# A selective-scan network on one core: the starting value of each bank of sums comes from ScalarE instead of TensorE

## The chip, the cores and the metric

The kernel runs on one NeuronCore of one Trainium2 chip. The metric is the device time in microseconds (us) of one execution of the whole network. One execution has also been taken by the hardware profiler; its trace gives start, length and releaser of every instruction. The engines are named PE (TensorE, matrix products), PEld (its weight loads), DVE (VectorE), ACT (ScalarE), POOL (GpSimd) and SP (the queue that issues most DMAs).

## What is computed

The network has four layers on a 4 x 56 x 56 x 96 image. Layers 0 and 1 are state-space layers: a 192-channel sequence of L = 3136 tokens is run through a selective scan in four directions (along the rows or along the columns, each forward and reversed), and the four results are added. Layers 2 and 3 are attention and a small feed-forward net. What matters here is the scan, cut from the reference:

```python
def step(h, inp):
    dA_l, dBu_l, C_l = inp
    h = dA_l * h + dBu_l                                  # per channel d and state n (16 states)
    return (h, jnp.einsum('bkdn,bkn->bkd', h, C_l))       # sum over the 16 states
_, ys = jax.lax.scan(step, h0, (dA, dBu, Ct))
return jnp.moveaxis(ys, 0, -1) + u * Dp[None, :, :, None] # the skip term
...
y = jnp.transpose(y1 + y2 + y3 + y4, (0, 2, 1)).reshape(Bsz, Hh, Ww, DINNER)
```

So for each direction a sum over 16 states is formed, the four directions are added up, and `u * D` is added (for all four directions at once it is `u` times the sum of the four D, in layer 0 weighted by a softmax).

## The kernel before

**Rounds.** The scans of the two layers, the four images, the four directions and the seven chunks of 448 tokens are one long list of *rounds* (`scans`, from line 604). A chunk has eight rounds, r = 0 to 7: two halves of the channels (e = 0, 1; 96 channels each) times four quarters of the states (q = 0 to 3). There are 2 x 4 x 4 x 7 x 8 = 1792 rounds. The order of the instructions is written out by hand: every engine runs its own list in the order in which Python emits it.

In one round n these are emitted:

- DVE: two products `h <- du, b` (line 695), then three scans (line 702), one for each group of 32 channels; further elementwise work of the other lanes stands between.
- ACT: three exponentials `da` into three PSUM banks (`decay`, line 654), each for the next round; group g can be written only when scan g of this round has read the bank. Two small copies carry the scan's state from chunk to chunk (`kept` line 672, `carried` line 667).
- POOL: one product `h <- du, cb` (line 690) and the product with C, `hc <- h, cb` (line 744).
- PE: `b`, the row of B spread over partitions (line 597, `begin`), for the next round. There is one bank for it, so it waits for this round's two products. Then `add_up` (line 764): four products of `hc` with a 0/1 matrix `four` (line 775), which add the sums over states of round n - 2 to the bank `y`. Two rounds lie between a scan and its sum: the list `late`.

**The bank `y`.** It gathers four rounds (q = 0 to 3), 96 channels x 448 tokens. There is one such bank. Before the change, `add_up` of q = 0 starts it: a product of the identity with Y (the running sum of the directions), or in the first direction of U with the diagonal matrix `skip` (line 771, `start=True`), which overwrites the bank. Two products with a zero matrix follow (line 772), then the four sums. After q = 3 `keep_sums` (line 779) copies the bank back to Y on ACT (line 782). Since `keep_sums` of one half and the start of the next use the same bank, line 771 waits for line 782. In terms of r, `keep_sums` stands in rounds r = 1 and r = 5, and the start of the next bank in r = 2 and r = 6. There are 448 such changes of bank.

**Directions.** In the directions along the columns (`orient` = 1) Y and U are read and written with a stride of 56 elements. Two of the four directions of each layer are of that kind; the first, which reads U, never is.

**Zeros.** `keep_busy` (line 754) puts products with a zero matrix on PE so that each round has about the same amount of work on it: `WARM` = 6.8 units less what the planner has counted for the round in `self.work`. It does nothing in the rounds with q = 0. It is called ahead of `begin`, so these zeros stand ahead of `b` in PE's list. They write into the bank `y`, adding nothing.

**The other lanes.** All other parts of the network (projections, convolutions, feed-forward nets) are generators that are advanced between the pieces of a round (`overlap`, line 935). A planner decides by `spend` and `room` (lines 965 and 973) whether a piece fits: it keeps a backlog for ACT and PE, reduced by `SPARE` each half round, and bounded by `ACT_LIMIT` and `PE_LIMIT`. The list `strided` (line 718) books the product of line 771 as 1.5 units of PE, or 3.0 in a strided direction. After the last round, what is left of the lanes runs alone (the *tail*).

Of the kernel before, what the change touches and what calls it, by code (L numbers as in the profile page):

```python
# [11 lines left out]
F32 = mybir.dt.float32  # L12
# [3 lines left out]
AF = mybir.ActivationFunctionType  # L16
# [4 lines left out]
HS = 56  # L21
L = HS * HS
C = 96
DI = 192
NS = 16
NE = 2
NG = 3
NQ = 4
# [4 lines left out]
CS = 448  # L33
# [16 lines left out]
WARM, PER_P = 6.8, 1.6  # L50
# [116 lines left out]
class Net:  # L167
# [82 lines left out]
    def setup(self):  # L250
        nc, tc, const = self.nc, self.tc, self.const
# [46 lines left out]
        w = const.tile([128, 4], F32, name="wts")  # L298
# [15 lines left out]
        for l in range(2):  # L314
            dv = par("c128", f"{l}D")[:C].rearrange("p (e k) -> p e k", e=NE)
            s = const.tile([C, NE], F32, name=f"dsum{l}")
            if l == 0:
                dw = const.tile([C, NE, 4], F32, name="dw")
                nc.vector.tensor_tensor(dw, dv, w[:C].unsqueeze(1).to_broadcast([C, NE, 4]), ALU.mult)
                dv = dw  # L320
            nc.vector.tensor_reduce(s, dv, AX.X, ALU.add)
            g = const.tile([C, NE, C], F32, name=f"skip{l}")
            for e in range(NE):
                nc.vector.tensor_scalar_mul(g[:, e], self.ident[:C, :C], s[:, e : e + 1])
            self.skip.append(g)


        bn = {}
        for n, bias in (("bn1", "1dw_b"), ("bn2", "1pw_b")):
            s = const.tile([C, 1], F32, name=n + "s")  # L330
# [273 lines left out]
    def scans(self):  # L604

        nc, sp = self.nc, self.sp
        chunks = []
        for l in range(2):
            for i in range(NB):
                for n, (orient, rev) in enumerate(ORDER[l]):
                    for step in range(NCS):
                        ch = Step()
                        ch.l, ch.i, ch.orient, ch.rev, ch.step = l, i, orient, rev, step
                        ch.k = 2 * orient + rev if l == 0 else orient + 2 * rev  # L620
                        ch.c = NCS - 1 - step if rev else step
                        ch.n, ch.first = n, n == 0 and step == 0
                        ch.skip = n == 0
                        ch.last = n == 3 and step == NCS - 1
                        ch.cb, ch.dt, ch.du = [], [], []
                        chunks.append(ch)
        rounds = [(ch, e, q) for ch in chunks for e in range(NE) for q in range(NQ)]
        per = NE * NQ


        da = [self.psum.tile([128, 512], F32, name=f"da{g}")[:, : CS + 4] for g in range(NG)]
        for t in da:
            nc.vector.memset(t, 0.0)

        def steps(n):

            return [(ch, n - per * j) for j, ch in enumerate(chunks[max(0, n // per) : n // per + 3], max(0, n // per))]

        def ahead(n):
            for ch, o in steps(n):  # L640
                self.on_tensor(ch, o)

        for n in range(-14, 0):
            for ch, o in steps(n):
                self.prepare(ch, o)
            for ch, o in steps(n):
                self.prepare_on_scalar(ch, o)
            ahead(n)

        def decay(n, g):  # L650

            if n < len(rounds):
                ch, e, q = rounds[n]
                nc.scalar.activation(da[g][:, INNER], ch.dt[e][:, g], AF.Exp, scale=ch.par.na[:, e, q, g : g + 1])  # L654

        def column(t, at):

            return t[:, at : at + 2 * ROW + 1 : ROW]

        def carried(n):  # L660

            if n < len(rounds):
                ch, e, q = rounds[n]
                hs[n] = sp.tile([128, WIDE], F32, name="h", bufs=3)
                if not ch.step:
                    return
                nc.scalar.copy(column(hs[n], ROW if ch.rev else 1), ch.par.carry[:, e, q])  # L667

        def kept(n):
            ch, e, q = rounds[n]  # L670
            if ch.step < NCS - 1:
                nc.scalar.copy(ch.par.carry[:, e, q], column(hs[n], 2 if ch.rev else CS + 1))  # L672

        def own(n):
            ch, e, q = rounds[n]
            return NQ * e + q in (OWN_TAIL if ch.l and ch.i else OWN)

        hs, bs = {}, {}

        def tokens(t):  # L680

            return self.groups(t, 2)[:, :, :CS]

        def begin(n):

            if n < len(rounds):
                ch, e, q = rounds[n]
                bs[n] = self.spread_b(ch, q)
                if not own(n):
                    nc.gpsimd.tensor_tensor(tokens(hs[n])[:, 2], ch.du[e][:, 2], ch.cb[q][:, 1], ALU.mult)  # L690

        def products(n):
            ch, e, q = rounds[n]
            for g in range(3 if own(n) else 2):
                nc.vector.tensor_tensor(tokens(hs[n])[:, g], ch.du[e][:, g], bs[n], ALU.mult)  # L695

        def scan(n, g):
            ch, e, q = rounds[n]
            c = 1 if ch.step else 0
            way = slice(CS + 1 + c, 1, -1) if ch.rev else slice(2 - c, CS + 2)  # L700
            h = hs[n][:, g * ROW :]
            nc.vector.tensor_tensor_scan(h[:, way], da[g][:, way], h[:, way], 0.0, ALU.mult, ALU.add)  # L702

        carried(0)
        carried(1)
        begin(0)
        self.exp_and_ln()
        self.tables = True
        for g in range(NG):
            decay(0, g)  # L710
        late = []
        for n, (ch, e, q) in enumerate(rounds):
            r = NQ * e + q
            products(n)
            for c, o in steps(n):
                self.prepare(c, o)
            self.half_round()
            strided = [1.5 + 1.5 * ch.orient] * (r % NQ == 2)
            strided += [1.5 + 1.5 * c.orient for c, o in steps(n) for _ in self.projected(c, o)]
            self.spend((0.6, 0.7, 1.7, 0, 0, 0, 0.7, 0.6)[r], (1.3, 1.3, 0, 0, 0, 0, 0.4, 0.4)[r] + sum(strided))  # L720
            yield "F", n, r
            for c, o in steps(n):
                self.prepare_on_scalar(c, o)
            ended = late.pop(0) if len(late) == 2 else None
            if ended:
                self.keep_busy(ended[2])
            begin(n + 1)
            if ended:
                self.add_up(*ended)
            ahead(n)  # L730
            self.half_round()
            for g in range(NG):
                if g == 1:
                    yield "C", n, r
                if g == 2 and ended and ended[2] == NQ - 1:
                    self.spend(0.6, 0)
                    self.keep_sums(*ended[:3])
                scan(n, g)
                if g == 2:
                    kept(n)  # L740
                decay(n + 1, g)
            carried(n + 2)
            hc = sp.tile([128, NG, CS], F32, name="hc", bufs=3)
            nc.gpsimd.tensor_tensor(  # L744
                hc, tokens(hs[n]), ch.cb[q][:, 0].unsqueeze(1).to_broadcast([128, NG, CS]), ALU.mult,
            )
            late.append((ch, e, q, hc))
            del hs[n], bs[n]
        for ended in late:
            self.add_up(*ended)  # L750
        self.keep_sums(ch, e, q)
        yield "C", len(rounds), 0

    def keep_busy(self, q):

        if q:
            self.add_zeros(int(max(0.0, WARM - self.work) + 0.5))
        self.work = 0.0

    def add_zeros(self, n):  # L760
        for _ in range(n):
            self.nc.tensor.matmul(self.y[:C], self.zeros, self.some, start=False, stop=False)  # L762

    def add_up(self, ch, e, q, hc):

        nc = self.nc
        if q == 0:
            self.y = self.psum.tile([128, 512], F32, tag="y", name="y", bufs=1)[:, :CS]
            o = self.y[:C].rearrange("p (a b) -> p a b", b=HS)
            a, w = (self.U[e], self.skip[ch.l][:, e]) if ch.skip else (self.Y[e], self.ident[:C, :C])  # L770
            nc.tensor.matmul(o, w, self.in_order(a, ch.orient, ch.c * CS, CS), start=True, stop=False)  # L771
            self.add_zeros(2)

        for n, g in enumerate((0, 1, 2, 2)):
            nc.tensor.matmul(  # L775
                self.y[32 * n : 32 * n + 32], self.four, hc[:, g], start=n == 3, stop=n == 3 or q == NQ - 1,
            )

    def keep_sums(self, ch, e, q):

# [591 lines left out]
```

## Time and profile before

| | us |
|---|---|
| median of 3 runs | 8356.53 (8340.41 to 8364.75) |
| the profiled execution, time | 8364.46 |
| the profiled execution, span from first to last instruction | 8362.7 |
| outside the span | 1.8 |
| first round starts / last scan ends (timeline) | 111.8 / 7983.9 |
| tail after the last scan | 378.8 |

| engine | busy us | share | instructions |
|---|---|---|---|
| PE | 7469.6 | 89% | 33633 |
| PEld | 2721.6 | 33% | 33633 |
| DVE | 7516.6 | 90% | 9555 |
| ACT | 6109.8 | 73% | 12807 |
| POOL | 7177.3 | 86% | 3991 |

A row of the page's table of groups names the source line, the engine, the operation, what it writes and reads (`out<-in`) and its shape; then the busy time in us and the mean length of one in ns; then the idle time of that engine just before these instructions and what ended most of it. A product of fp32 operands shows as two records in this trace (14336 records of line 775 for 1792 x 4 products). The mean granted clock of PE is 0.898 of full speed; in the record it is either full or half.

### The profile page before, as it was taken

The page shows a single profiled execution, that of the slowest core. Times are in us where ns is not written, and L with a number is a line of the kernel's source. Part 1 is how long each engine was busy: PE and PEld are TensorE (multiplying, and loading weights), DVE is VectorE, ACT ScalarE, POOL GpSimd, SP SyncE. Part 2 cuts the span into 40 slices and gives each one's busy share as a digit, 9 for nine tenths or more (in the row PEclk, how much of TensorE's full clock was granted, in tenths as well). Part 3 has the DMA queues.
Part 4 walks back from the last instruction along what each step waited for, and adds up shares of the span by engine and source line. Part 5 has one row for each costly group of instructions (what it writes and reads, how often), then busy time and mean ns, then how long its engine had stood idle before and what let it go on. Part 6 is the DMA issues. An engine that isn't in the chain of part 4 may idle for free. (4 is left out here: it accounts for less than half of the span.)

```text
span 8362.7 us, 119228 instructions
## 1 busy us (share of the span) xinstructions
PE 7469.6 (89%) x33633; PEld 2721.6 (33%) x33633; DVE 7516.6 (90%) x9555; ACT 6109.8 (73%) x12807; POOL 7177.3 (86%) x3991
## 2 busy tenths in 40 slices
PE   7889888898889988898899979988899888998997
PEld 3333233232333223232322323333333333333344
DVE  5999999999998999999998999999999999999921
ACT  5778878776787768786777766777776777767736
POOL 4999989989998999899898998998888888889820
PEclk8899989899999989998898989988899888999986
DMA  5777777678766777677776777676766667666721
GB/s 154 179 188 189 203 179 182 167 175 199 178 174 170 172 188 181 172 177 184 177 175 167 174 185 176 166 170 172 186 166 162 166 173 182 167 160 167 175 57 48
DMA packets 944159, 1417.77 MB, mean 170 GB/s; under 512 B 169410, under 2 KB 936644, under 8 KB 942628
## 3 DMA queue, kind: packets, MB, share of 16 engines
q1 hardware_dynamic: 942720, 1408.34, 68.2%
q8 instruction: 264, 4.33, 0.2%
q14 instruction: 403, 3.30, 0.1%
q10 hardware_dynamic: 772, 1.80, 0.1%
HBM read 1141.42 MB, written 268.14 MB: 169 GB/s over the span
## 5 line engine op out<-in xcount | busy, mean ns | idle before, releaser
L702 DVE TENSOR_TENSOR_SCAN h<-da,h 128x449 f32<-128x449 f32 (+1 forms) x5376 | 5507.1, 1071 | 134.9 <-ACT da L654 79.3
L744 POOL TENSOR_TENSOR hc<-h,cb 128x1344 f32<-128x1344 f32 x1792 | 4884.8, 2726 | 598.8 <-DVE h L702 413.6
L654 ACT ACTIVATE da<-dt,na 128x448 f32<-128x448 f32 x5376 | 3353.1, 632 | 1143.2 <-DVE h L702 1104.4
L695 DVE TENSOR_TENSOR h<-du,b 128x448 f32<-128x448 f32 x3584 | 2019.6, 604 | 182.7 <-PE b L597 112.6
L775 PE MATMUL y<-hc,four 128*32 128x448 f32 x14336 | 1913.0, 609 | 17.8 <-POOL hc L744 17.4
L690 POOL TENSOR_TENSOR h<-du,cb 128x448 f32<-128x448 f32 x1792 | 1754.1, 979 | 141.4 <-DMA cb<-cd 110.1
L762 PE MATMUL y<-w,zeros 128*96 128x448 bf16 x4843 | 1354.0, 397 | 0.0
L597 PE MATMUL b<-cf,sel 128*128 128x448 bf16 x1792 | 680.2, 380 | 631.2 <-DVE h L695 626.6
L762 PEld LDWEIGHTS <-zeros 128*96 128x96 bf16 x4843 | 603.2, 135 | 1111.0 <-issue 965.1
L775 PEld LDWEIGHTS y<-hc,four 128*32 128x32 f32 x14336 | 294.2, 113 | 1182.5 <-issue 660.5
L433 PE MATMUL pp<-U,wd 96*128 96x448 f32 x896 | 664.5, 830 | 12.1 <-DMA U<-u 8.3
L771 PE MATMUL y<-Y,ident 96*96 96x448 f32 x672 | 542.9, 898 | 18.6 <-ACT Y L782 14.3
L919 PE MATMUL ps<-win,dg 64*64 64x220 f32 (+11 forms) x1998 | 547.3, 471 | 0.0
L479 PE MATMUL pp<-cf,wd 12*96 12x448 f32 (+1 forms) x896 | 476.2, 613 | 71.7 <-ACT dtc L489 47.6
L672 ACT COPY carry<-h 128x3 f32<-128x3 f32 x1536 | 301.9, 197 | 282.3 <-DVE h L702 276.2
L504 POOL TENSOR_TENSOR duc<-dtc,U 96x896 f32<-96x896 f32 x224 | 483.1, 2157 | 3.3 <-ACT dtc L491 3.3
L782 ACT COPY Y<-y 96x448 f32<-96x448 f32 x448 | 341.7, 763 | 77.7 <-PE y L775 76.8
L919 PEld LDWEIGHTS ps<-win,dg 64*64 64x64 f32 (+2 forms) x1998 | 239.7, 162 | 321.5 <-issue 289.0
L667 ACT COPY h<-carry 128x3 f32<-128x3 f32 x1536 | 280.2, 182 | 66.3 <-POOL hc L744 63.5
L489 ACT ACTIVATE dtc<-pp,wd 96x448 f32<-96x448 f32 x448 | 281.7, 629 | 31.3 <-PE pp L479 27.4
L597 PEld LDWEIGHTS <-sel 128*128 128x128 bf16 x1792 | 183.8, 103 | 336.1 <-issue 272.7
L827 PEld LDWEIGHTS ps<-avg,w 96*112 96x112 f32 (+2 forms) x1944 | 249.9, 193 | 108.1 <-issue 59.0
(427 smaller groups left out, 5933.9 us busy)
## 6 DMA issues: line engine op xcount, KB each, us to landing
cb<-cd SPq DMA_DIRECT2D x3584, 112.0 KB, 3.9
dt<-dd SPq DMA_DIRECT2D x1792, 168.0 KB, 4.3
du<-dd SPq DMA_DIRECT2D x1792, 168.0 KB, 4.1
dd<-dtc SPq DMA_DIRECT2D x224, 336.0 KB, 3.0
dd<-duc SPq DMA_DIRECT2D x224, 336.0 KB, 3.1
U<-u SPq DMA_DIRECT2D x112, 168.0 KB, 4.7
z<-w SPq DMA_DIRECT2D x56, 224.0 KB, 4.5
u<-w SPq DMA_DIRECT2D x56, 224.0 KB, 3.9
```

The costliest lines, as they stand in the source:

```text
L433: self.nc.tensor.matmul(ch.ps.rearrange("p (a b) -> p a b", b=HS), ch.par.wx[:, e], self.in_order(self.U[e], ch.orient, ch.c * CS, CS), st ...
L504: self.nc.gpsimd.tensor_tensor(in_rows(ch.duc), in_rows(ch.dtc), u[:, :, lo : lo + CS // HS], ALU.mult)
L597: self.nc.tensor.matmul(ps, self.sel[:, q], self.upper(ch.cf), start=True, stop=True)
L654: nc.scalar.activation(da[g][:, INNER], ch.dt[e][:, g], AF.Exp, scale=ch.par.na[:, e, q, g : g + 1])
L690: nc.gpsimd.tensor_tensor(tokens(hs[n])[:, 2], ch.du[e][:, 2], ch.cb[q][:, 1], ALU.mult)
L695: nc.vector.tensor_tensor(tokens(hs[n])[:, g], ch.du[e][:, g], bs[n], ALU.mult)
L702: nc.vector.tensor_tensor_scan(h[:, way], da[g][:, way], h[:, way], 0.0, ALU.mult, ALU.add)
L744: nc.gpsimd.tensor_tensor(hc, tokens(hs[n]), ch.cb[q][:, 0].unsqueeze(1).to_broadcast([128, NG, CS]), ALU.mult,)
L762: self.nc.tensor.matmul(self.y[:C], self.zeros, self.some, start=False, stop=False)
L771: nc.tensor.matmul(o, w, self.in_order(a, ch.orient, ch.c * CS, CS), start=True, stop=False)
L775: nc.tensor.matmul(self.y[32 * n : 32 * n + 32], self.four, hc[:, g], start=n == 3, stop=n == 3 or q == NQ - 1,)
L919: self.nc.tensor.matmul(o[:, a - r0 : e - r0, x0:x1], diag[:, tap], win[:, a + dy - lo : e + dy - lo, x0 + dx : x1 + dx], start=n == 0, st ...
```

## The change

The bank is no longer started by PE. `begin_sums`, called straight after `keep_sums`, has ACT write the starting value into the bank: a copy of Y, or U scaled by a column of the sums of D. The four sums of q = 0 then add to it like those of the other quarters. Once, at the beginning, a product of zeros with `start=True` is issued to the bank. The diagonal matrices `skip` are not built any more. `keep_busy` now works in the rounds with q = 0 too, so up to seven zeros stand ahead of `b` there instead of two behind it. The planner no longer books the product of line 771; for the new ACT instruction nothing is booked.

```diff
@@ setup
-            g = const.tile([C, NE, C], F32, name=f"skip{l}")
-            for e in range(NE):
-                nc.vector.tensor_scalar_mul(g[:, e], self.ident[:C, :C], s[:, e : e + 1])
-            self.skip.append(g)
+            self.skip.append(s)
@@ scans
             decay(0, g)
+        self.begin_sums(*rounds[0][:2], True)
...
-            strided = [1.5 + 1.5 * ch.orient] * (r % NQ == 2)
-            strided += [1.5 + 1.5 * c.orient for c, o in steps(n) for _ in self.projected(c, o)]
+            strided = [1.5 + 1.5 * c.orient for c, o in steps(n) for _ in self.projected(c, o)]
...
                 if g == 2 and ended and ended[2] == NQ - 1:
                     self.spend(0.6, 0)
                     self.keep_sums(*ended[:3])
+                    self.begin_sums(*rounds[n - 1][:2])
                 scan(n, g)
@@ keep_busy, add_zeros, add_up
-        if q:
-            self.add_zeros(int(max(0.0, WARM - self.work) + 0.5))
+        self.add_zeros(int(max(0.0, WARM - self.work) + 0.5))
         self.work = 0.0
...
-        nc = self.nc
-        if q == 0:
-            self.y = self.psum.tile([128, 512], F32, tag="y", name="y", bufs=1)[:, :CS]
-            o = self.y[:C].rearrange("p (a b) -> p a b", b=HS)
-            a, w = (self.U[e], self.skip[ch.l][:, e]) if ch.skip else (self.Y[e], self.ident[:C, :C])
-            nc.tensor.matmul(o, w, self.in_order(a, ch.orient, ch.c * CS, CS), start=True, stop=False)
-            self.add_zeros(2)
-
         for n, g in enumerate((0, 1, 2, 2)):
-            nc.tensor.matmul(
+            self.nc.tensor.matmul(
                 self.y[32 * n : 32 * n + 32], self.four, hc[:, g], start=n == 3, stop=n == 3 or q == NQ - 1,
+                skip_group_check=True,
             )
+
+    def begin_sums(self, ch, e, first=False):
+
+        self.y = self.psum.tile([128, 512], F32, tag="y", name="y", bufs=1)[:, :CS]
+        if first:
+            self.nc.tensor.matmul(self.y[:C], self.zeros, self.some, start=True, stop=True)
+        o = self.y[:C].rearrange("p (a b) -> p a b", b=HS)
+        a = self.in_order((self.U if ch.skip else self.Y)[e], ch.orient, ch.c * CS, CS)
+        if ch.skip:
+            self.nc.scalar.activation(o, a, AF.Copy, scale=self.skip[ch.l][:, e : e + 1])
+        else:
+            self.nc.scalar.copy(o, a)
```

More of the change, by code (lines that the diff above doesn't have):

```diff
@@ L761, in add_zeros @@
         for _ in range(n):
-            self.nc.tensor.matmul(self.y[:C], self.zeros, self.some, start=False, stop=False)
+            self.nc.tensor.matmul(self.y[:C], self.zeros, self.some, start=False, stop=False, skip_group_check=True)
     def add_up(self, ch, e, q, hc):
-        nc = self.nc
-        if q == 0:
-            self.y = self.psum.tile([128, 512], F32, tag="y", name="y", bufs=1)[:, :CS]
-            o = self.y[:C].rearrange("p (a b) -> p a b", b=HS)
-            a, w = (self.U[e], self.skip[ch.l][:, e]) if ch.skip else (self.Y[e], self.ident[:C, :C])
-            nc.tensor.matmul(o, w, self.in_order(a, ch.orient, ch.c * CS, CS), start=True, stop=False)
-            self.add_zeros(2)
         for n, g in enumerate((0, 1, 2, 2)):
-            nc.tensor.matmul(
+            self.nc.tensor.matmul(
                 self.y[32 * n : 32 * n + 32], self.four, hc[:, g], start=n == 3, stop=n == 3 or q == NQ - 1,
+                skip_group_check=True,
             )
+    def begin_sums(self, ch, e, first=False):
[8 more added lines that the diff above has]
+            self.nc.scalar.copy(o, a)
     def keep_sums(self, ch, e, q):
```

## The prediction, made before the changed kernel ran

> **What bounds the kernel now.** I read the page first, then the busy times up to the last scan and after it, then DVE's waits, then one change of bank in the timeline.
>
> ```profile
> L702 DVE TENSOR_TENSOR_SCAN h<-da,h 128x449 f32<-128x449 f32 (+1 forms) x5376 | 5507.1, 1071 | 134.9 <-ACT da L654 79.3
> L654 ACT ACTIVATE da<-dt,na 128x448 f32<-128x448 f32 x5376 | 3353.1, 632 | 1143.2 <-DVE h L702 1104.4
> ```
> ```profile
> 112.00:7984.00 7872.00, 7071.74 (x31972) 2486.09 (x31972) 7443.78 (x9367) 5857.82 (x12269) 7136.16 (x3946) 0.91 0.71 176
> 7984.00:8362.70 378.70, 321.93 (x1411) 192.08 (x1410) 53.42 (x102) 200.52 (x460) 30.92 (x28) 0.75 0.17 46
> ```
> ```profile
> DVE h L695 <- PE b L597: 112.6, 143, 4.6
> DVE h L702 <- ACT da L654: 79.3, 165, 2.1
> DVE h L702 <- POOL h L690: 53.2, 26, 10.1
> DVE h L695 <- DMA du<-dd: 34.4, 9, 15.6
> DVE w L856 <- PE ps L842: 24.2, 14, 3.7
> ```
>
> In the windows the columns are length, PE, PEld, DVE, ACT, POOL, clock, DMA share, GB/s. DVE is busy for 7444 of the 7872 us of the rounds: it is the bound, and only 428 us of its idle time can be won. ACT mostly waits for DVE (1104 us before `da`): it has room on average, 26%. The largest of DVE's waits is for `b`, 112.6 us. In the tail DVE works 53 of 379 us; PE, at a clock of 0.75, is busy 322.
>
> A change of bank, in a strided direction (start, length):
>
> ```profile
> 884.44 0.99 ACT L782 COPY Y<-y 96x448 f32<-96x448 f32 x1
> 884.74 1.12 DVE L695 TENSOR_TENSOR h<-du,b 128x448 f32<-128x448 f32 x2
> ...
> 885.28 0.65 ACT L654 ACTIVATE da<-dt,na 128x448 f32<-128x448 f32 x1
> 885.78 3.05 DVE L702 TENSOR_TENSOR_SCAN h<-da,h 128x449 f32<-128x449 f32 x3
> ...
> 885.91 0.36 PE L597 MATMUL b<-cf,sel 128*128 128x448 bf16 x1 [1.85 <-DVE h L695]
> ...
> 886.11 1.81 PE L771 MATMUL y<-Y,ident 96*96 96x448 f32 x2
> ...
> 887.74 0.93 PE L762 MATMUL y<-w,zeros 128*96 128x448 bf16 x2
> ...
> 888.59 1.72 PE L775 MATMUL y<-hc,four 128*32 128x448 f32 x8
> 888.75 1.12 DVE L695 TENSOR_TENSOR h<-du,b 128x448 f32<-128x448 f32 x2
> ```
>
> The round takes 888.75 - 884.74 = 4.01 us, set by DVE alone (two products, three scans). `b` for the next round is done at 886.27, 2.5 us before it is needed, because nothing stands ahead of it. Then the clock falls: two zeros take 0.93 us and the four sums 1.72, against 0.96 in rounds at full clock. The clock record has 265 half-clock stretches between first and last round, 1481 us in all; 110 start in r = 2 and 62 in r = 6, the two rounds without zeros, 93 in the other six.
>
> **What the Trainium skill says.** "TensorE: Matmul & The Clock Gate", section "What's actually happening": PE's clock is full or half, decided by a free-running window of 3.4 us. The record agrees: 157 of the 265 stretches last 3.4 us, 73 last 6.8. "PSUM — Partial Sum Buffer", section "The four PSUM rules": writes of ScalarE leave the bits alone that decide whether a product adds or overwrites, so a seed needs them set by an earlier product. The one product with `start=True` at the beginning does that, and no later one with `start=True` touches the 96 partitions: the change does what it says. No trace of before shows it. "ScalarE: Activation LUTs", section "What ACT_TABLE_LOAD costs": an operand of one value per partition adds about 93 ns. The trace has 523 ns for a copy of `cf` (L474) and 626 with such a scale (L472): 103 ns.
>
> **The change part by part.**
>
> *ACT gains 448 instructions.* A contiguous copy of 448 columns takes 0.52 us, a scaled one 0.63 (the same rows of `cf`); a strided one 1.02, by the Y copy in strided directions. That row writes with a stride to SBUF, while the new one reads with it. Bounds: 0.52, if a strided read is free, to 1.02; line 771's record is 987 ns strided and 539 contiguous (the median of Y, and of U), so strided reads double on PE, and I take 1.02. With 112 scaled, 112 contiguous, 224 strided: 70.6 + 58.2 + 228.5 = 357 us on ACT, 6110 to 6467. Queued behind each are `kept`, the third `da`, `carried`. In the example that `da` ends at 886.9 instead of 885.9, and scan 3 wants it at 887.8: hidden. Where ACT runs late (lane pieces ahead of it) it isn't. Shifting ACT's instructions at each change of bank until its idle gaps absorb the shift, and setting each `da` against its scan: 62 us in all.
>
> *PE: zeros ahead of `b`, behind ACT.* By the order of the built lists the new kernel has 5767 zeros, 4843 before; in r = 2 there are 5.1 on average ahead of `b` (6.1 in layer 0), in r = 6 3.5, and none before. They write the bank, so the first waits for the new ACT write, and `b` is queued behind them; DVE's products wait for `b`. In the example: write done at 885.4 + 1.0 = 886.4; six zeros at full clock, 0.2 us each (spacing in the timeline), to 887.6; `b` 0.36, to 888.0, wanted at 888.75. Hidden by 0.7 us. At half clock a zero takes 0.37 to 0.40 and `b` 0.57: 886.4 + 2.4 + 0.6 = 889.4, late by 0.65. The cover is gone where the clock is half or ACT late. The same sum at all 448 changes, with the clock that the record has there, and the later of `da` and `b`:
>
> | direction, clock when the zeros start | changes | DVE late, us |
> |---|---|---|
> | contiguous, full | 167 | 9 |
> | contiguous, half | 55 | 44 |
> | strided, full | 162 | 47 |
> | strided, half | 62 | 63 |
> | sum (two at the ends left out) | 446 | 163 |
>
> This counts each change alone. Part is absorbed by later waits of DVE that would come anyhow (POOL, DMA); I take a fifth, as such waits are 88 of 428 us: -33, leaving 130. Bounds: 56 (`b` at full clock everywhere) to 163.
>
> *PE loses line 771 and two zeros*, 664 us busy in all. After `b` the four sums follow at once; comparing with the old end at each change, PE is done 1.0 us earlier on average. Where DVE now waits for the `b` after it, up to that much goes: 44 of the 112.6 us. Its waits for other products (`ps`, five rows, 73 us) fall too; I take a fifth, 15 (bounds 0 and 40). What is late next is ACT.
>
> *The planner.* Without the booked 1.5 or 3.0 units it lets lane work in earlier. In the built order DVE has 91 instructions after the last scan, not 103; PE 857, not 946; 18 feed-forward pieces instead of 21. The tail's timeline has fourteen such pieces from 8121 to 8280 and seven from 8282 to 8360: 11.4 and 11.1 us each. Three fewer and one attention fewer, a few conv taps more: -35. The moved work costs DVE some 5 us in the rounds: -30 net (bounds -15, -37).
>
> *Setup:* four DVE products of the diagonals and one start product; under 2 us of 112, nothing.
>
> Sum: +130 - 44 - 15 - 30 = +41 on the profiled 8364.5 gives 8405. The median of the runs shown is 8 us lower, and one of them took 8364.75; I take 8400.
>
> **The rivals.**
>
> 1. *The clock stays up (faster).* If zeros in r = 2 and r = 6 bring these rounds' drops to the level of the others, 172 stretches become about 31. The half-clock rows lose all but some 15 of 107 us: lateness is 71, four fifths of it 57. DVE idles 141 us in half-clock time, 79 more than its share by rounds; two thirds of it, 52, go. 57 - 44 - 15 - 30 - 52 = -84: 8280. Between +41 at 265 stretches and -84 at 124 the sum is zero at about 220; below that it decides. For it: that is where the drops are. Against it: zeros can't start before ACT's write, 0.7 (contiguous) to 1.7 us (strided) after the round's start; PE is idle until then as now until `b` at 1.1; and the work in r = 2 is about 1.2 (zeros) + 0.36 + 0.96 = 2.5 us, against 2.8 with a contiguous line 771 and 3.8 with a strided one. PE isn't busier, only otherwise spread.
> 2. *Relief and lateness cancel.* With the 56 us bound, without clock gains: 45 - 44 - 15 - 30 = -44; with the new strided write at 0.52, less. With half the half-clock lateness it is about zero: 8355. For it: in layer 0, chunks with strided directions are not slower than the others now, though their Y copy is 0.5 us longer on ACT.
> 3. *It compounds.* Longer idle time ahead of the zeros in strided rounds drops the clock oftener; each drop makes zeros and `b` late, and ACT's unbooked 357 us pushes lane work and `da`: all 163 and half as much again, little relief: +245 - 44 - 0 - 30 - 60 (absorbed) = +110: 8475.
>
> **How the numbers follow.** `b` late behind ACT and zeros (8400, own range 8370 to 8450): 0.46. Rival 1: 0.24, rival 2: 0.18, rival 3: 0.12. The range 8270 to 8465 leaves out the lower part of rival 1 and half of rival 3. A measurement tells about 0.3%, 25 us, from no change. Faster: 0.21 of rival 1 and 0.04 of rival 2, 0.25. Same: 0.03 of rival 1, 0.12 of rival 2, 0.05 of the forecast, 0.20. Slower: 0.41 of the forecast, 0.12 of rival 3, 0.02 of rival 2, 0.55.
>
> **What would show it.** DVE's wait for `b` grows to 150 to 220 us, sitting in rounds r = 3 and 7 and following half clock; its wait for `da` to 100 to 140. ACT is busy near 6470 us, the strided write near 1.0 us. The tail is near 345 us. The forecast is wrong if the half-clock stretches fall under about 220 (rival 1), or if strided writes take 0.5 us.

## The result and the profile after

The changed kernel takes 8429.7 us (median of 4 runs, 8423.8 to 8432.8) against 8360.6 before: ratio 1.0089, 95% interval 1.0072 to 1.0106. That is slower by 0.9%, on the side that was forecast with 0.55, and 30 us over the forecast of 8400.

The page's rows, of the changed kernel, that answer to those shown of before:

```profile
PE 7243.5 (86%) x33661; PEld 2729.8 (32%) x33661; DVE 7524.1 (89%) x9551; ACT 6477.7 (77%) x13255; POOL 7181.8 (85%) x3991
...
L699 DVE TENSOR_TENSOR_SCAN h<-da,h 128x449 f32<-128x449 f32 (+1 forms) x5376 | 5512.5, 1071 | 181.8 <-ACT da L651 127.7
...
L651 ACT ACTIVATE da<-dt,na 128x448 f32<-128x448 f32 x5376 | 3341.8, 631 | 1059.2 <-DVE h L699 1022.9
L692 DVE TENSOR_TENSOR h<-du,b 128x448 f32<-128x448 f32 x3584 | 2019.5, 604 | 222.6 <-PE b L594 163.9
L759 PE MATMUL y<-w,zeros 128*96 128x448 bf16 x5766 | 1606.0, 409 | 418.2 <-ACT y L779 355.3
```

DVE's work is what it was (7524 us, 7517 before). What grew is idle time just before the scans (127.7 us for `da`, 79.3 before) and before the products (163.9 us for `b`, 112.6 before). The zeros have a wait that no zero had before: 355 us for ACT's write of the bank. Their row of before ends in no idle time at all:

```profile
L762 PE MATMUL y<-w,zeros 128*96 128x448 bf16 x4843 | 1354.0, 397 | 0.0
```

ACT is busy 368 us more; 357 was the estimate.

The durations of ACT's instructions on the bank (minimum, median, maximum in ns):

```profile
L784 ACT COPY Y<-y x448: 518/754/1032, 137.8 to 8096.1; 96x448 f32<-96x448 f32 x150
L779 ACT COPY y<-Y x336: 532/998/1041, 360.6 to 8083.7; 96x448 f32<-96x448 f32 x168
L777 ACT ACTIVATE y<-U,dsum x112: 616/634/636, 111.9 to 7313.3; 96x448 f32<-96x448 f32 x112
```

So a strided read costs ACT what a strided write does, 1.0 us against 0.53. The busy times of the rounds and of the tail, columns as before (length, PE, PEld, DVE, ACT, POOL, clock, DMA share, GB/s):

```profile
113.50:8092.10 7978.60, 6879.72 (x32114) 2509.39 (x32114) 7457.25 (x9379) 6242.05 (x12762) 7143.82 (x3949) 0.89 0.70 174
8092.10:8429.20 337.10, 286.37 (x1296) 175.98 (x1294) 48.34 (x91) 183.53 (x413) 27.83 (x25) 0.78 0.17 47
```

The rounds are 106.5 us longer (7872.1 before) and the tail 41.8 shorter (378.9). And one change of bank in a strided direction, of the changed kernel, at the same kind of place as the one shown of before:

```profile
865.94 0.99 ACT L784 COPY Y<-y 96x448 f32<-96x448 f32 x1
866.24 1.12 DVE L692 TENSOR_TENSOR h<-du,b 128x448 f32<-128x448 f32 x2
866.96 1.00 ACT L779 COPY y<-Y 96x448 f32<-96x448 f32 x1
...
868.01 2.77 PE L759 MATMUL y<-w,zeros 128*96 128x448 bf16 x7 [2.45 <-ACT y L779]
...
870.58 0.58 PE L594 MATMUL b<-cf,sel 128*128 128x448 bf16 x1
...
871.20 1.15 DVE L692 TENSOR_TENSOR h<-du,b 128x448 f32<-128x448 f32 x2 [0.87 <-PE b L594]
```

This is the mechanism in six rows; the square brackets give how long the engine sat idle before the row, and for what. The two copies on ACT end at 867.96. The first of seven zeros had waited 2.45 us for that. The clock is at half by then, so the seven take 2.77 us. `b` comes behind them, and DVE, which could have gone on at 870.33, waits 0.87 us.

The next table sums DVE's idle time in the rounds by what ended it, and for `b` by the round in which it was computed (us; the half-clock stretches have their number and total length). These sums, and those of the table of experiments, lie up to 2 us beside the rows of the views:

| | idle | `da` | `b` | `b` in r = 2 and 6 | `b` in the other six | other products of PE | half clock |
|---|---|---|---|---|---|---|---|
| before | 428 | 80 | 114 | 25 | 88 | 104 | 265, 1481 |
| after | 521 | 129 | 165 | 118 | 47 | 104 | 290, 1707 |

In the chunks that run along the rows the rounds took 3923 us before and 3932 after; in the strided ones 3941 and 4039 (each pair adds up to 8 us less than the rounds). Nearly all of the loss is there. It also goes with the clock: of the 118 us for `b` in r = 2 and 6, some 104 lie at changes of bank where `b` itself ran at half clock. And of the growth of `da`, some 38 us are waits of the third scan in r = 2 and 6, whose `da` stands right behind ACT's write.

### The profile page after: what moved, and what is told of

Its sections match the earlier page's. It is cut to its first block, busy times and chain, and to the rows that moved or that the text cites. A ratio compares the mean times of both kernels' runs of the same rounds, so it can differ in the third digit from the quotient of the medians.

```text
span 8429.2 us, 119751 instructions
## 1 busy us (share of the span) xinstructions
PE 7243.5 (86%) x33661; PEld 2729.8 (32%) x33661; DVE 7524.1 (89%) x9551; ACT 6477.7 (77%) x13255; POOL 7181.8 (85%) x3991
## 4 chain that ended last, share of the span: by engine, by line
PE 30%; ACT 23%; DVE 21%; issue 10%; POOL 7%; DMA 7%; SPq 1%; DVEq 0%; POOLq 0%; ACTq 0%
DVE h L699 15%; ACT da L651 7%; PE y L764 6%; PE y L759 5%; POOL hc L742 5%; DVE h L692 4%; PE ps L921 4%; ACT Y L784 3%; DMA cb<-cd 2%; PE b L594 2%; ACT y L779 2%; DMA du<-dd 2%; PE ps L829 2%; PE pp L476 2%; PE pp L430 1%
## 5 line engine op out<-in xcount | busy, mean ns | idle before, releaser
L699 DVE TENSOR_TENSOR_SCAN h<-da,h 128x449 f32<-128x449 f32 (+1 forms) x5376 | 5512.5, 1071 | 181.8 <-ACT da L651 127.7
L692 DVE TENSOR_TENSOR h<-du,b 128x448 f32<-128x448 f32 x3584 | 2019.5, 604 | 222.6 <-PE b L594 163.9
L759 PE MATMUL y<-w,zeros 128*96 128x448 bf16 x5766 | 1606.0, 409 | 418.2 <-ACT y L779 355.3
L759 PEld LDWEIGHTS <-zeros 128*96 128x96 bf16 x5766 | 734.2, 137 | 1450.8 <-issue 1247.3
L594 PE MATMUL b<-cf,sel 128*128 128x448 bf16 x1792 | 711.1, 397 | 469.9 <-DVE h L692 464.1
L476 PE MATMUL pp<-cf,wd 12*96 12x448 f32 (+1 forms) x896 | 494.3, 634 | 76.4 <-ACT dtc L486 43.2
L921 PE MATMUL ps<-win,dg 64*64 64x220 f32 (+9 forms) x1980 | 527.9, 466 | 0.0
L829 PEld LDWEIGHTS ps<-avg,w 96*112 96x112 f32 (+1 forms) x1984 | 261.0, 198 | 115.1 <-issue 62.4
L779 ACT COPY y<-Y 96x448 f32<-96x448 f32 x336 | 285.4, 849 | 10.7
L565 ACT COPY cf<-pp 64x448 f32<-64x448 f32 x448 | 235.6, 526 | 48.6 <-PE pp L587 39.8
```

Of the source, the lines that this page charges most:

```text
L476: self.nc.tensor.matmul(ch.pd, ch.par.wt[rows, C * e : C * e + C], ch.cf[rows], start=True, stop=True)
L594: self.nc.tensor.matmul(ps, self.sel[:, q], self.upper(ch.cf), start=True, stop=True)
L921: self.nc.tensor.matmul(o[:, a - r0 : e - r0, x0:x1], diag[:, tap], win[:, a + dy - lo : e + dy - lo, x0 + dx : x1 + dx], start=n == 0, st ...
```

## The experiments

Each time is a median, with the ratio to the kernel before, run on the same chip (its medians there were 8347 to 8361), and the 95% interval. Runs were taken on several chips, so they are compared by their ratios. The sums over the rounds are of one profiled execution each, up to 16 us away from the median of its run; differences of that size between sums mean little. They stand together here:

| run | time, us | ratio (interval) | rounds | tail | `da` | `b` | `b` in r = 2, 6 | rows / strided chunks |
|---|---|---|---|---|---|---|---|---|
| before | 8360.6 | | 7872 | 379 | 80 | 114 | 25 | 3923 / 3941 |
| after | 8429.7 | 1.0089 (1.0072, 1.0106) | 7979 | 337 | 129 | 165 | 118 | 3932 / 4039 |
| e1_b_first | 8396.1 | 1.0048 (1.0032, 1.0063) | 7930 | 345 | 157 | 85 | 28 | 3931 / 3991 |
| e2_two_zeros | 8381.8 | 1.0027 (1.0016, 1.0037) | 7906 | 355 | 172 | 68 | 14 | 3907 / 3991 |
| e3_before_act_write | 8490.2 | 1.0163 (1.0146, 1.0180) | 8011 | 379 | 151 | 118 | 10 | 3936 / 4067 |
| e4_booking | 8384.1 | 1.0030 (1.0018, 1.0042) | 7876 | 379 | 173 | 83 | 26 | 3926 / 3942 |
| e5_booking_same_zeros | 8396.5 | 1.0056 (1.0041, 1.0072) | 7906 | 375 | 147 | 134 | 86 | 3925 / 3973 |
| e6_contiguous | 8358.8 | 1.0007 (0.9996, 1.0017) | 7892 | 344 | 100 | 137 | 90 | 3916 / 3968 |
| e8_late_write | 8422.4 | 1.0084 (1.0065, 1.0102) | 7963 | 354 | 104 | 122 | 23 | 3935 / 4020 |
| e9_late_write_booking | 8370.9 | 1.0025 (1.0012, 1.0039) | 7881 | 376 | 128 | 110 | 18 | 3918 / 3955 |
| p1_before_no_booking | 8390.9 | 1.0049 (1.0033, 1.0065) | 7941 | 344 | 71 | 117 | 25 | 3937 / 3996 |
| h1_rows_on_act | 8360.7 | 1.0020 (1.0011, 1.0029) | 7871 | 364 | 88 | 92 | 19 | 3938 / 3925 |
| h2_rows_on_act_booking | 8363.8 | 1.0019 (1.0010, 1.0028) | 7863 | 378 | 91 | 105 | 27 | 3926 / 3929 |
| s1_swap_alone | 8352.6 | 1.0004 (0.9993, 1.0015) | 7874 | 374 | 168 | 59 | 18 | 3922 / 3944 |

### e1_b_first: `b` ahead of the zeros

```diff
-            if ended:
+            if ended and ended[2]:
                 self.keep_busy(ended[2])
             begin(n + 1)
+            if ended and not ended[2]:
+                self.keep_busy(ended[2])
```

> The changed kernel with one pair of lines exchanged: in rounds r = 2 and r = 6 b stands ahead of the zeros, so it no longer waits for ACT's write; number of zeros, ACT's writes and planner unchanged. Theory (b waits behind zeros that wait for ACT's write): DVE's wait for b in r = 2 and 6 falls from 118 us to about 25, its wait for da stays near 129, time 8430 - 90 = 8340 (8320 to 8370). Rival A (ACT's 357 us more are the cost): wait for b falls, but da and the waits for other products take it up, 8400 to 8430. Rival B (the planner's missing booking): 8420 to 8440.

Measured 8396, 34 us less, not 90: outside the ranges of the theory and of rival A, and nearer to the latter. The wait for `b` in r = 2 and 6 fell from 118 to 28 us as expected, but `da` rose from 129 to 157. DVE's waits in this run:

```profile
DVE h L699 <- ACT da L651: 155.9, 241, 3.3
DVE h L692 <- PE b L594: 84.2, 98, 3.5
```

Once `b` was there, more of DVE's idle time went to `da`. So the place of the zeros costs some 34 us in this setting, under half of the growth of that wait.

### e2_two_zeros: the round is not filled

```diff
-        self.add_zeros(int(max(0.0, WARM - self.work) + 0.5))
+        if q:
+            self.add_zeros(int(max(0.0, WARM - self.work) + 0.5))
...
+        if q == 0:
+            self.add_zeros(2)
         for n, g in enumerate((0, 1, 2, 2)):
```

> The changed kernel without the zeros that fill the rounds of q = 0: b first, then two zeros behind it, as in the kernel before, now behind ACT's write. Theory: b is free as in e1, so about e1's time, 8340, within 20 us; PE is less busy in these rounds, so if the fill of zeros keeps the clock up, half-clock stretches rise from e1's number by over 40 and this run is slower than e1 by 20 us or more; if the fill does nothing, the two agree within 10 us. Rival A: 8400 to 8430, no less than e1.

Measured 8382, some 40 us over what I expected. It has 303 half-clock stretches to e1's 274, 29 more where a working fill was to bring over 40, and yet it isn't slower than e1: the two medians differ by 14 us the other way. The mean clock is 0.885 in e1 and 0.873 here; whatever the higher clock is worth, the zeros that bring it cost as much or more. That the sums and the lanes' products come sooner with fewer zeros is a likely reason, not a tested one. `da` takes up what `b` gives here too:

```profile
DVE h L699 <- ACT da L651: 171.5, 272, 2.1
DVE h L692 <- PE b L594: 67.2, 64, 3.8
```

### e3_before_act_write: ACT's write without any gain

```diff
...
                     self.keep_sums(*ended[:3])
+                    self.begin_sums(*rounds[n - 1][:2])
...
+    def begin_sums(self, ch, e):
+        self.y = self.psum.tile([128, 512], F32, tag="y", name="y", bufs=1)[:, :CS]
+        o = self.y[:C].rearrange("p (a b) -> p a b", b=HS)
+        a = self.in_order((self.U if ch.skip else self.Y)[e], ch.orient, ch.c * CS, CS)
+        self.nc.scalar.copy(o, a)
```

> The kernel before, with ACT's write into the bank added after the copy to Y; PE's product then overwrites it, so all of before's PE work stays and b is not behind the write. It is ACT's 350 us alone. Theory: da waits rise from 80 to about 125 us, b waits somewhat since line 771 starts later: 8361 + 45 = 8405 (8385 to 8425). Rival A (ACT is the whole cost): 8440 or more. If ACT's write costs nothing: 8360 within 10.

Measured 8490: 133 us, three times what I expected and with rival A. In the rounds, DVE's wait for `da` grew by 70 us, and those for other products of PE and ACT by 25 each. Line 771 (772 in this run) had to wait for the longer pair of copies, and what stands behind it on PE came later. Its row before, and in this run:

```profile
L771 PE MATMUL y<-Y,ident 96*96 96x448 f32 x672 | 542.9, 898 | 18.6 <-ACT Y L782 14.3
L772 PE MATMUL y<-Y,ident 96*96 96x448 f32 x672 | 557.4, 919 | 81.1 <-ACT y L785 78.4
```

So the price is not only that `da` comes later on ACT: part of it reaches DVE through PE. Of the 139 us added to the rounds, 126 lie in strided chunks, where the write takes 1.0 us and line 771 two records of 0.99. DVE's longest waits:

```profile
DVE h L702 <- ACT da L654: 147.7, 259, 2.5
DVE h L695 <- PE b L597: 116.2, 128, 3.5
DVE h L702 <- POOL h L690: 54.4, 27, 10.3
```

`da` is late 259 times in place of 165, none of them by more than 2.5 us: many small delays, not a few long ones.

### e4_booking and e5_booking_same_zeros: the planner

e4 puts the booking of the removed product back; booked work also lowers the number of zeros (4541, against 5767 in the changed kernel). e5 puts it in the backlog alone (5831 zeros).

```diff
@@ e4
-            strided = [1.5 + 1.5 * c.orient for c, o in steps(n) for _ in self.projected(c, o)]
+            strided = [1.5 + 1.5 * ch.orient] * (r % NQ == 2)
+            strided += [1.5 + 1.5 * c.orient for c, o in steps(n) for _ in self.projected(c, o)]
@@ e5
+            self.backlog[1] += (1.5 + 1.5 * ch.orient) * (r % NQ == 2)
             yield "F", n, r
```

> The changed kernel with the planner's booking of the removed product put back (1.5 or 3.0 units in r = 2 and 6), so lane work comes in as late as before and fewer zeros are issued in these rounds. Theory: the tail grows back from 337 to about 375 us, the rounds lose little, 10 to 30 us from fewer zeros ahead of b: 8430 + 38 - 20 = 8448 (8430 to 8465). Rival B (lane work let in too early is what made the rounds slower): rounds fall by 60 us or more, 8400 or less.

> The changed kernel with the removed product booked in the planner's backlog alone, not in the count that sets the zeros: lane work comes in as late as before, while r = 2 and 6 keep their zeros ahead of b. It splits e4 (8384), which had both. If the zeros ahead of b are what e4 took away: b waits stay near 165 us, the tail grows to 379, 8440 to 8470. If the lane work let in early is the cost: rounds fall by about 100 us as in e4, 8380 to 8395.

Both are faster than the changed kernel, by 0.59 and 0.33% in ratio. e4 missed my theory's 8448 and came out with rival B. e5 is next to its second case (8380 to 8395), though its rounds lose 72 us and not 100. The tail grows by 38: the lane work that the planner lets in early costs about twice in the rounds what it saves in the tail. In e4 the rounds come down another 30 us with the fewer zeros ahead of `b` (its wait in r = 2 and 6 falls from 86 to 26), though `da` rises by 26. In e5 DVE's waits are:

```profile
DVE h L699 <- ACT da L651: 145.2, 241, 2.7
DVE h L692 <- PE b L594: 132.0, 157, 3.4
```

Against 127.7 and 163.9 in the changed kernel: with the lane work later, `b` waits 32 us less and `da` 18 us more. The rest of the gain is in the waits for other products of PE (29 us less) and for ACT's other outputs (13 less).

### p1_before_no_booking: the same in the kernel before

```diff
-            strided = [1.5 + 1.5 * ch.orient] * (r % NQ == 2)
-            strided += [1.5 + 1.5 * c.orient for c, o in steps(n) for _ in self.projected(c, o)]
+            strided = [1.5 + 1.5 * c.orient for c, o in steps(n) for _ in self.projected(c, o)]
```

> The kernel before with the planner's booking of line 771 taken out and nothing else: the product itself stays. e5 put the booking back in the changed kernel and its rounds fell by 72 us while the tail grew by 38. If lane work let in early costs in any kernel: rounds here rise by 50 to 90 us, the tail falls by 35, 8370 to 8410. If it costs only where ACT is short of room: rounds rise by 20 us or less, 8325 to 8345.

Measured 8391: slower by 0.49%, with no change but what the planner believes and what it does in consequence (it lets lane work in earlier and issues 107 zeros fewer). The rounds grow by 69 us, the tail falls by 35, as in the first case of the expectation. The windows of its rounds and tail:

```profile
112.50:8053.30 7940.80, 7101.58 (x31980) 2489.89 (x31980) 7449.42 (x9379) 5885.96 (x12315) 7139.23 (x3949) 0.90 0.71 175
8053.30:8397.10 343.80, 295.15 (x1296) 182.39 (x1296) 48.36 (x91) 183.61 (x413) 27.89 (x25) 0.76 0.17 46
```

DVE has 12 instructions more in the rounds and 6 us more to do (7449 us; 7444 before), so the work that moves to DVE isn't what costs. It is the waits around it. Of this run:

```profile
DVE w L1149 <- PE ps L1147: 33.4, 18, 4.5
DVE h L695 <- ACT da L654: 27.4, 22, 1.7
DVE h L695 <- ACT carry L672: 12.6, 10, 2.9
DVE h L695 <- ACT h L667: 8.9, 3, 3.6
```

In the kernel before the same four were 13.5, 1.6, 3.5 and 1.4 us. (Line 695 doesn't read `da`; the view names what came last on ACT.) Together, waits on products of PE other than `b` grew by 15 us and those on ACT's outputs other than `da` ahead of a scan by 46; 42 of these stand before the products of line 695. The half-clock time also grew, from 1481 to 1570 us, but three quarters of the added waits are put down to ACT and not to PE.

### e6_contiguous: the same writes, half as long where strided

```diff
-        a = self.in_order((self.U if ch.skip else self.Y)[e], ch.orient, ch.c * CS, CS)
+        a = self.in_order((self.U if ch.skip else self.Y)[e], 0, ch.c * CS, CS)
```

> The changed kernel with ACT's write reading in a row in all directions, so that 224 of 448 writes take 0.53 instead of 1.0 us; in these the starting value is that of other tokens, so the sums are not the reference's. It takes 105 us off ACT and nothing else. ACT as the limit (da waits 129 us, b waits behind the write): both fall, -40 to -80 us, 8350 to 8390. If the length of the write is hidden and only its place in the order of waits costs: within 15 of 8430.

Measured 8359, 71 us less. The copy takes 0.53 us everywhere:

```profile
L779 ACT COPY y<-Y x336: 532/532/534, 363.0 to 7996.4; 96x448 f32<-96x448 f32 x168
```

This takes 224 x 0.466 = 104 us off ACT, and DVE waits 20 to 30 us less for each of `da`, `b` and PE's other products. Two thirds of what is taken off the strided writes thus reach the end in the changed kernel. And with these short writes nearly nothing is left of its loss (ratio 1.0007), though the zeros still fill the round and the booking is still dropped.

### e8_late_write and e9_late_write_booking: the write moved back

e8 is e1 with the write behind the third `da`; e9 adds e4's booking.

```diff
-                    self.begin_sums(*rounds[n - 1][:2])
...
             carried(n + 2)
+            if ended and ended[2] == NQ - 1:
+                self.begin_sums(*rounds[n - 1][:2])
```

> e1 (b ahead of the zeros) with ACT's write moved behind the third da and the carried copy of the round. If da is late because the write stands ahead of it: da waits fall from 157 us to about 100, b stays near 85, 8396 - 50 = 8345. If ACT's total work is the cost, wherever it stands: da stays near 150 and shifts to the next round, 8385 to 8410.

> e8 with the planner's booking of e4 (fewer zeros, lane work as late as before). If both help independently: 8340 - 20 = 8320, under the kernel before (8357). If e4's gain was b alone, which e8 has already: as e8 in the rounds, tail longer by about 35 us, 8360 to 8385.

e8 missed both theories: 8422, against 8396 for e1. `da` did fall by 53 us, but the wait for `b` rose by 37 and that for other products by 34, probably because the sums and all that stands behind them on PE started later. e9, with the booking, is at 8371; its ratio, 1.0025, can't be told from e4's 1.0030. The time is that of its second case, but not for the reason given there: its rounds are 82 us shorter than e8's. Moving the write here passed the wait from one engine to the other.

### h1_rows_on_act and h2_rows_on_act_booking: ACT where it is cheap

`begin_sums` returns early in the strided directions, and the product with the identity is back there, booked as before; the zeros don't fill the round. In h2 the product of the other directions, which is gone, is booked too.

```diff
...
+        if q == 0:
+            if ch.orient:
+                o = self.y[:C].rearrange("p (a b) -> p a b", b=HS)
+                a = self.in_order(self.Y[e], ch.orient, ch.c * CS, CS)
+                self.nc.tensor.matmul(o, self.ident[:C, :C], a, start=True, stop=False, skip_group_check=True)
+            self.add_zeros(2)
...
+        if ch.orient:
+            return
```

> ACT starts the bank only in the directions along the rows (224 of 448 changes, writes of 0.52 and 0.63 us); in the strided ones line 771 does, as before. b first, two zeros behind it; strided products booked, row ones not. All the loss of the changed kernel lay in the chunks of strided directions (3941 to 4039 us, rows 3923 to 3932). If the strided write is the cost: strided chunks back near 3941, rows 3905 to 3925, tail some 20 us shorter, 8325 to 8350. If ACT's write costs in itself: 8365 or more.

> h1 with the row products still booked, as in the kernel before: fewer lane pieces and zeros early. If booking is worth in the rounds what it costs in the tail here: within 10 us of h1. If early lane work is what costs: 15 to 30 us under h1, 8310 to 8335.

8361 and 8364: 0.2% over the kernel before, both. h1 lies between its two cases. In h2 the booking makes no difference that can be seen (3 us), as in its first. The strided chunks are back (3925 and 3929), but the row chunks gain nothing. No version that I tried beats the kernel before.

### s1_swap_alone: the swap without the fill and with the booking

e2 and e4 together: ACT's write takes the place of line 771, all else as in the kernel before. To the changed kernel:

```diff
-        self.add_zeros(int(max(0.0, WARM - self.work) + 0.5))
+        if q:
+            self.add_zeros(int(max(0.0, WARM - self.work) + 0.5))
...
+        if q == 0:
+            self.add_zeros(2)
...
+            strided = [1.5 + 1.5 * ch.orient] * (r % NQ == 2)
+            strided += [1.5 + 1.5 * c.orient for c, o in steps(n) for _ in self.projected(c, o)]
```

> The swap alone: ACT's write in place of line 771, with the planner's booking and the zeros (two, behind b) as in the kernel before. Of the changed kernel's 69 us, the zeros ahead of b (e2: -48, e1: -34) and the missing booking (e5: -34) would be gone. If they add up: 8350 to 8365, strided chunks within 20 us of before's 3941. If what one leaves the wait for da takes up: 8370 to 8390, da waits 150 us or more, and the strided write is then a cost by itself.

Measured 8353, ratio 1.0004 (0.9993 to 1.0015): no difference. Its waits:

```profile
DVE h L699 <- ACT da L651: 167.8, 258, 2.7
DVE h L692 <- PE b L594: 59.1, 53, 4.6
```

Against before, `b` waits 54 us less and `da` 88 more; smaller waits make up most of the rest, and the rounds are 7874 us (7872 before). Half of the expectation's second case is in it, `da` at 168, but the time is that of the first. From this run the changed kernel is reached in two steps that nearly add up, in per cent over the kernel before:

| | zeros as before | zeros fill the round |
|---|---|---|
| booking kept | 0.04 (s1) | 0.56 (e5) |
| booking dropped | 0.27 (e2) | 0.89 (the change) |

The swap by itself costs nothing that can be measured, the fill of zeros ahead of `b` about 0.5 to 0.6%, the dropped booking 0.2 to 0.3%. This is one way to divide the loss, not the only one. Dropping the booking also added to the zeros, and e4, which keeps the booking in both respects and fills the round with what is left, is at 0.30. And e6 loses next to nothing with both steps taken. Its writes are shorter, which holds the zeros up less and also takes 104 us off ACT; no run tells these two apart.

## Why the prediction was right, and where not

The direction and its main reason held. Point by point:

- *ACT's 448 writes, 357 us, strided 1.0 us.* Measured 356 us (285 and 71), 998 ns. Right.
- *`b` late behind zeros behind the write, and `da` late: 163, of which 130 remain.* With the planner as before, e5 shows `b` in r = 2 and 6 up by 60 us and `da` by 67: 127. This is lateness before anything is absorbed, so it answers to the 163. DVE's waits for what isn't PE or `da` (POOL, DMA, ACT's other outputs, idle time without a releaser) fell by some 28 us, near the 33 that were taken as absorbed, which leaves about 99 and not 130. The cause was right and the size a quarter too large. That it would follow half clock was right (104 of 118 us). `da` was expected at 100 to 140 us and `b` at 150 to 220: 127.7 and 163.9.
- *`b` freed by the removed product: -44.* In the other six rounds `b` fell from 88 to 47 us, -41. Right. (The 664 us given for line 771 and two zeros are line 771's alone; the sum doesn't use them.)
- *Other products of PE: -15.* In e5 -28; in the changed kernel 0, where lane work comes early.
- *The tail: -35.* Measured -42, with 91 DVE instructions in it. Right.
- *The planner: -30 net, the moved work costing 5 us in the rounds.* This is the step that failed. By p1 it costs 69 us in the rounds for 35 in the tail, and by e5 72 for 38: +34, not -30. I had priced the moved work by DVE's own instructions, which indeed grew by some 6 us; the waits that it brings were left out. Swapping that term, +34 in place of -30, turns the sum from +41 into +105. The measured +66.5 of the profiled spans is under that, since in e5 the rest came to +34 in the rounds and not to the +71 (130 - 44 - 15) of the prediction: the lateness was some 31 us smaller than taken, and the relief of PE's other products 13 larger. Two errors of opposite sign, 64 and 37 us, hid each other in part. That the sum came within 30 us is partly luck.
- *Rival 1, the clock stays up.* Refuted: stretches starting in r = 2 are 111 (110 before), in r = 6 45 (62), and 290 in all (265). The reason given against it holds in the rows above: PE sat idle 2.45 us before the zeros. Nor does their number decide: s1 has 301 stretches at a mean clock of 0.877, and is 0.85% faster by the ratios than the changed kernel with 290. The clock matters where zeros stand ahead of `b`, as the 104 us show.
- *Rival 2, relief and lateness cancel.* That is what the swap does by itself (s1); the fill and the booking are what break the balance. I had put it at 0.18 for the change as a whole.
- *Rival 3, it compounds.* The time lies between the forecast and this rival's 8475. Half-clock time did grow, from 1481 to 1707 us, but the stretches that were added start outside r = 2 and 6 (134 there, 93 before), so the chain that it names isn't what is seen. Of its parts, the lane work that is pushed is the one that p1 and e5 show.

What stays open: whether the zeros cost some 0.2% even when they stand behind `b` (e1 against e2, whose intervals overlap), and why. In e2 the sums stand behind two zeros instead of three to five on average; that the later sums are the reason is argued, not shown. No run booked ACT's new write in the planner's backlog, so what that omission costs is not known.

## What to carry to other kernels

An instruction that only fills time should not wait for another engine ahead of one that is on the critical path. Here the fill behind ACT's write cost half a per cent, most of it because it stood ahead of `b` (0.89% with the zeros there, 0.48 with the same zeros behind `b`, 0.27 without the fill). When work is taken off an engine under a planner, its booking is a second change; try the two apart, since the freed room gets filled and what fills it brings waits, not only work. And a swap that takes from one busy engine and gives to another can move the wait rather than remove it: here 54 us less for `b` came with 88 more for `da`.

## What was not expected of the hardware

A copy of 96 x 448 fp32 on ACT took 998 ns where it read SBUF with a stride of 56 elements, and 532 ns where it read in a row. The prediction had only been able to take this from the strided write, which costs the same. And filling the rounds with zeros, with the booking kept, raised the mean clock from 0.877 (s1) to 0.893 (e5), while the time rose by 0.5%: a higher clock on PE was no gain here, since the zeros that brought it stood in the way.
